# Preln attention with a mixture of experts: the last blocks' weighted sums turned by VectorE and DMA for three of eight token blocks

## The chip, the cores and the metric

The kernel runs on one core of one Trainium2 chip. The metric is the device time of one launch in microseconds (us), the median of several runs of the same program. TensorE (PE) multiplies matrices, VectorE (DVE), ScalarE (ACT) and GpSimd (POOL) work on rows, and SP only issues DMA transfers. Each engine takes its instructions in the order of the built program and waits on semaphores.

## The reference

Input x has 4096 tokens of width 256, in float32. Two residual steps follow each other:

```python
x = x + attention(layernorm(x), Qw, Kw, Vw)        # causal, one head of width 256
x = x + moe(layernorm(x))

h      = x @ W_in + b_in
probs  = softmax(h @ W_gate + b_gate)              # 8 experts, the best 2, shares normalized
mid    = relu(h @ W1[e] + b1[e])                   # 256 -> 1024
eout   = mid @ W2[e] + b2[e]                       # 1024 -> 256
out    = (share0 * eout0 + share1 * eout1) @ W_out + b_out
```

## The kernel before, in words

Tokens are cut into 8 blocks of 512 (NB blocks of TB), each of 4 tiles of 128 rows (TPB). The first half of the program is the attention, block by block. The second half gathers the rows of each expert from DRAM, computes `mid` and `eout` for groups of rows in one long list of work (`work`), and scatters each row's result to a DRAM array `parts`, two rows for a token, by indirect DMA on GpSimd's queue (line 997, in `contribute`). The last group of that list is called z: its rows are those of one expert from the last two token blocks.

The change concerns the end, where each token's two results are fetched, weighted, summed and multiplied by W_out. Four functions do it for a block b:

- `collect(b)` (line 1155) issues the loads of the block's rows from `parts` on SP's queue: two tiles `yp` of 512 KB (four of 256 KB for block 0). The two tiles use the buffers of pools `kt` and `v`, 8 each, in which the experts' weights were.
- `add_up(b)` (line 1170) makes the weighted sums `acc`, for each tile of 128 rows one product on ScalarE (line 1175) and one multiply-add on VectorE (line 1177).
- `gather(b)` (line 1187) calls `add_up` for every block but 0, turns the sums by 8 transposes of 128x128 on TensorE into two PSUM tiles `pa` (line 1195), and copies these by ScalarE into two tiles `aT` (line 1200). Here width runs along the partitions, as the next product wants it.
- `leave(b, aT)` (line 1203) multiplies by W_out, 2 matmuls for each of the 4 tiles, into PSUM tiles `pf` (line 1209), of which there are 4; VectorE adds the residual (line 1217, `ot`), and SP issues the output (line 1222; line 1219 for the last block).

A float32 matmul appears as two records in the profile, a float32 transpose as one.

The loads of blocks 0 to 5 are issued while the last group z is computed. Blocks 6 and 7 need z's scattered rows, so their loads come after it; SP's queue is in order, so everything issued later on SP stands behind them. Then the loop runs: `gather(b + 1)`, `leave(b)`. The order of instructions is that of the calls where they are pinned (`pin` and `keep_in_program_order` fix an instruction's place after the one before it on its engine); elsewhere a scheduler that estimates durations sets it when the program is built. In the program before, it interleaves the transposes of block b + 1 with the matmuls of block b on TensorE, and the sums of block b + 1 with the output additions of block b on VectorE.

In the attention part some blocks of layer-normed rows are already turned without TensorE: `turn_todo` (line 323) transposes 32x32 squares in place on VectorE, two instructions of 128x512 (line 329), and then moves the squares to their partitions by 16 transfers of 32 KB on SP's queue (line 334).

SP's transfers take eight completion semaphores in turn. Each issue waits until the last transfer on its semaphore has landed. GpSimd's queue does the same with eight of its own.

Of the kernel before, what the change touches and what calls it, by code (L numbers as in the profile page):

```python
# [10 lines left out]
F32 = mybir.dt.float32  # L11
# [6 lines left out]
P = 128  # L18
EPS = 1e-5
MASKED = -1e38  # L20
TB = 512
# [7 lines left out]
SQ = 32  # L29
LATE = 2  # L30
# [7 lines left out]
def preln_attention_moe_kernel(  # L38
# [249 lines left out]
    def first_rows():  # L288

        todo, keep = [], tc.keep_in_program_order  # L290
        z = ln_rows(0, 0, todo)
        for i in range(TPB // 2):
            for j in range(2):
                ln_stats(0, 2 * i + j, keep)
            ln_rstd(0, i, 2, keep)
        for do in todo:
            keep(do())
        return z
# [21 lines left out]
            for q in range(P // SQ)  # L320
        ]

    def turn_todo(zT, z):

        def stand(i):
            on = z[:, ts(i, TPB // 2), :]
            return nc.vector.transpose(on, on)

        def move():
            for q in range(P // SQ):
                for f in range(P // SQ):
                    nc.sync.dma_start(
                        out=zT[ts(f, SQ), :, :, ts(q, SQ)].rearrange("p j c i -> p (j c) i"),
                        in_=z[ts(q, SQ)].rearrange("p j (c f) -> p (j c) f", f=P)[
                            :, :, ts(f, SQ)
                        ],
                    )

        return [partial(stand, i) for i in range(2)] + [move]
# [7 lines left out]
    share = [const.tile([P, NT], F32, tag=f"share{k}", name=f"share{k}") for k in range(TOPK)]  # L349
# [123 lines left out]
    qT = {}  # L473
# [412 lines left out]
    def pin(done):  # L886
        if steady:
            tc.keep_in_program_order(done)
# [127 lines left out]
    z, gates = first_rows(), []  # L1016
# [62 lines left out]
    for g in range(NT // KU):  # L1079
        b, q = divmod(g, QPB)  # L1080
# [58 lines left out]
        if q == QPB - 1:  # L1139
            ln_rstd(1, b)  # L1140
            z1T = attn.tile([P, TPB, ND, P], F32, tag="z1T", name=f"z1T{b}", bufs=1)
# [8 lines left out]
                    do()  # L1150

    HT = TPB // 2
    yps, accs = {}, {}

    def collect(b):

# [10 lines left out]
                    tc.add_to_no_dep_group("out", get.ins)  # L1167
            yps[b, i] = yp

    def add_up(b):  # L1170
        for i in range(2):
            acc = accs[b, i] = piece(f"acc{b}_{i}", HT, D)
            for j in range(HT):
                t = b * TPB + i * HT + j
                pin(nc.scalar.mul(acc[:, j, :], yps[b, i][:, j, 0, :], share[0][:, t : t + 1]))
                pin(
                    nc.vector.scalar_tensor_tensor(
                        acc[:, j, :],
                        yps[b, i][:, j, 1, :],
                        share[1][:, t : t + 1],  # L1180
                        acc[:, j, :],
                        ALU.mult,
                        ALU.add,
                    )
                )

    def gather(b):

        pts = [ps_tr(f"pa{b}_{c}") for c in range(ND)]
        if b > 0:  # L1190
            add_up(b)
        for i in range(2):
            for j in range(HT):
                for c in range(ND):
                    nc.tensor.transpose(
                        pts[c][:, ts(i * HT + j, P)], accs[b, i][:, j, ts(c, P)], ident
                    )
        aT = [piece(f"aT{b}_{c}", TB) for c in range(ND)]
        for c in range(ND):
            nc.scalar.copy(aT[c], pts[c])  # L1200
        return aT

    def leave(b, aT):
        for i in range(2):
            ot = piece(f"ot{b}_{i}", HT, D)
            for j in range(HT):
                pf = ps_mm(f"pf{b}_{i}_{j}")
                for c in range(ND):
                    nc.tensor.matmul(  # L1209
                        pf[:, :D],  # L1210
                        lhsT=aT[c][:, ts(i * HT + j, P)],
                        rhs=wout_sb[:, c, :],
                        start=(c == 0),
                        stop=(c == ND - 1),
                    )
                t = i * HT + j
                nc.vector.tensor_tensor(ot[:, j, :], pf[:, :D], xb[b][:, t, :], ALU.add)
                if b == NB - 1:
                    nc.sync.dma_start(out=outs[b * TPB + t], in_=ot[:, j, :])
            if b < NB - 1:  # L1220
                t = b * TPB + i * HT
                nc.sync.dma_start(out=outs[t : t + HT].rearrange("t p d -> p t d"), in_=ot)
# [5 lines left out]
    for n, item in enumerate(work):  # L1228
        steady = n >= AHEAD
        if n == AHEAD:  # L1230
            take_late()
            quarters_left = nc.values_load(
                tables["d"][3][:1, :1],
                min_val=0,
                max_val=2 * NPAIR,
                skip_runtime_bounds_check_because="the sum of the experts' quarters",
            )

        if n + AHEAD + 1 < len(work):
# [13 lines left out]
        following = None  # L1253
        if n + 2 < len(work):
            following, behind = hidden(work[n + 1], got[n + 1], hTs.pop(n + 1), behind)
        if n == 0:
            turn(1, NB - 1, rows1, z1T)
            lg = enter(NB - 1, z1T, attn)
        if n == 1:
            seen = route(NB - 1, lg, seen, attn)  # L1260
            tables["z"], seen = plan_late(seen, early)
            tables["b"] = plan("b", seen, NBLK - NFULL, SB, SQR - 1, tables["a"][2])

            def twice(k):
                taken = const.tile([P, NE], F32, tag="twice" + k, name="twice" + k)
                nc.vector.tensor_scalar_mul(taken, tables[k][2], 2.0)
                return taken

            tables["c"] = plan("c", seen, NHALF, SH, SQR - 1, twice("b"))
            tables["d"] = plan("d", seen, 2 * NPAIR, SQR, SQR - 1, twice("c"))  # L1270
        if n == len(work) - 1:

            for b in range(NB - LATE):
                collect(b)
            add_up(0)
        contribute(item, got.pop(n), mid)
# [12 lines left out]
    steady = False  # L1289
    for b in range(NB - LATE, NB):  # L1290
        collect(b)

    aT = gather(0)
    for b in range(NB):
        following = gather(b + 1) if b + 1 < NB else None
        leave(b, aT)
        aT = following


# [30 lines left out]
```

## Time and profile before

| what | value |
| --- | --- |
| median of 3 runs | 1080.48 us (1079.9 to 1081.41) |
| the profiled execution's own time | 1071.75 us |
| its span, first to last instruction | 1070.0 us |
| granted TensorE clock | 1.000 |
| TensorE busy | 1062.3 us, 99% |
| VectorE busy | 674.6 us, 63% |
| last multiplication group z, first weighted sums | from 1017.25 us, from 1024.8 us |
| products with W_out (pf) | 1032.7 to 1066.4 us |

The profile is of one execution, whose own time is 8.7 us below the median of the runs. The span starts with its first instruction, and all positions are in us from there. A row of the chain gives start, length, engine, tile and line. A row of a tile's answer gives line, engine, operation, count, and the shortest, median and longest duration in ns. A row of SP's waits gives the line that waited, what for, the total in us, how often, and the longest. "Idle before" an instruction is in square brackets in a timeline, with what ended it.

In the end stretch, the busy time in each 8 us is:

```
us               PE    DVE   ACT   POOL  DMA share
1022 to 1030     8.00  2.10  3.33  0.98  0.99
1030 to 1038     7.43  3.80  4.64  0.98  1.05
1038 to 1046     8.00  5.94  5.15  0.00  0.99
1046 to 1054     8.00  5.81  4.67  0.00  0.73
1054 to 1062     8.00  6.22  4.67  0.00  0.37
1062 to 1070     4.80  2.55  0.62  0.00  0.38
```

### The profile page before, as it was taken

The page shows a single profiled execution, that of the slowest core. Times are in us where ns is not written, and L with a number is a line of the kernel's source. Part 1 is how long each engine was busy: PE and PEld are TensorE (multiplying, and loading weights), DVE is VectorE, ACT ScalarE, POOL GpSimd, SP SyncE. Part 2 cuts the span into 40 slices and gives each one's busy share as a digit, 9 for nine tenths or more (in the row PEclk, how much of TensorE's full clock was granted, in tenths as well). Part 3 has the DMA queues.
Part 4 walks back from the last instruction along what each step waited for, and adds up shares of the span by engine and source line. Part 5 has one row for each costly group of instructions (what it writes and reads, how often), then busy time and mean ns, then how long its engine had stood idle before and what let it go on. Part 6 is the DMA issues. An engine that isn't in the chain of part 4 may idle for free.

```text
span 1070.0 us, 15770 instructions
## 1 busy us (share of the span) xinstructions
PE 1062.3 (99%) x4973; PEld 882.9 (83%) x4973; DVE 674.6 (63%) x2114; ACT 332.4 (31%) x730; POOL 236.9 (22%) x289
## 2 busy tenths in 40 slices
PE   9999999999999999999999999999999999999998
PEld 6788888888888888888888887777778787777887
DVE  5877667564655546254665724858588786767636
ACT  2232233322432323242402221232323332323254
POOL 2104043103103000201222522232322322313110
PEclk9999999999999999999999999999999999999999
DMA  9422211121011011001655475887889896969285
GB/s 313 104 54 44 58 25 51 17 54 24 6 45 25 8 21 39 3 1 21 202 170 180 124 248 180 280 266 268 279 269 315 262 333 213 335 211 327 77 300 187
DMA packets 177995, 158.80 MB, mean 148 GB/s; under 512 B 82158, under 2 KB 157875, under 8 KB 177909
## 3 DMA queue, kind: packets, MB, share of 16 engines
q1 hardware_dynamic: 168980, 139.67, 42.4%
q0 software_dynamic: 8384, 17.58, 5.1%
q8 instruction: 40, 0.66, 0.3%
q10 hardware_dynamic: 544, 0.52, 0.1%
q14 instruction: 47, 0.38, 0.1%
HBM read 124.79 MB, written 26.38 MB: 141 GB/s over the span
## 4 chain that ended last, share of the span: by engine, by line
PE 97%; DVE 2%; POOL 0%; DMA 0%; issue 0%; SPq 0%; ACT 0%; DVEq 0%; POOLq 0%
PE po L633 21%; PE ps L555 21%; PE pm_a L921 11%; PE pe_a L988 11%; PE pe_b L988 5%; PE pm_b L921 5%; PE ph L362 3%; PE pm_c L951 3%; PE pf L1209 3%; PE pe_c L988 3%; PE pq L511 3%; PE pv L526 2%; PE pe_d L988 2%; PE pm_d L951 2%; PE pm_z L921 1%; PE pe_z L988 1%
## 5 line engine op out<-in xcount | busy, mean ns | idle before, releaser
L633 PE MATMUL po<-v,s 128*128 128x257 f32 x1056 | 237.9, 380 | 0.0
L555 PE MATMUL ps<-qT,zT 128*128 128x256 f32 x1088 | 233.3, 374 | 0.0
L555 PEld LDWEIGHTS ps<-qT,zT 128*128 128x128 f32 x1088 | 203.1, 190 | 28.0 <-issue 1.0
L633 PEld LDWEIGHTS po<-v,s 128*128 128x128 f32 x1056 | 197.2, 190 | 26.7
L564 ACT COPY s<-ps 128x512 f32<-128x512 f32 x120 | 70.2, 585 | 171.9 <-PE ps L555 132.6
L988 PE MATMUL pe_a<-w_a,mid_a 128*128 128x256 f32 x544 | 121.6, 380 | 0.0
L921 PE MATMUL pm_a<-hT_a,w_a 128*128 128x256 f32 x544 | 120.0, 379 | 0.0
L988 PEld LDWEIGHTS pe_a<-w_a,mid_a 128*128 128x128 f32 x544 | 102.6, 190 | 19.0 <-issue 5.6
L570 DVE TENSOR_TENSOR mx<-ps,mx 128x512 f32<-128x512 f32 x91 | 62.9, 691 | 83.7 <-ACT s L564 82.9
L930 ACT ACTIVATE mid_a<-pm_a,c_a 128x256 f32<-128x256 f32 x136 | 64.2, 472 | 165.1 <-PE pm_a L921 150.4
L921 PEld LDWEIGHTS pm_a<-hT_a,w_a 128*128 128x128 f32 x544 | 103.4, 190 | 14.1
L615 ACT ACTIVATE s<-s 128x512 f32<-128x512 f32 x120 | 72.2, 630 | 100.2 <-DVE s L612 100.2
L901 DVE STREAM_TRANSPOSE hT_a<-h_a 32x128 f32<-32x128 f32 x272 | 82.2, 302 | 3.8
L443 POOL DMA_INDIRECT slots<-assign,ati x64 | 62.5, 977 | 77.5 <-DVE ati L441 58.7
L612 DVE TENSOR_TENSOR s<-s,pmax 128x512 f32<-128x512 f32 x120 | 73.0, 679 | 7.3 <-PE pmax L608 7.3
L997 POOL DMA_INDIRECT parts<-y_a,slot_a x34 | 34.2, 1005 | 167.4 <-DVE y_a L996 138.0
L893 DVE STREAM_TRANSPOSE mid_c<-raw_c 32x256 f32<-32x256 f32 x128 | 55.8, 436 | 1.9
L988 PE MATMUL pe_b<-w_b,mid_b 128*128 128x256 f32 x256 | 56.8, 380 | 0.0
L921 PE MATMUL pm_b<-hT_b,w_b 128*128 128x256 f32 x256 | 56.6, 379 | 0.0
L988 PEld LDWEIGHTS pe_b<-w_b,mid_b 128*128 128x128 f32 x256 | 48.5, 190 | 9.4 <-issue 2.8
L921 PEld LDWEIGHTS pm_b<-hT_b,w_b 128*128 128x128 f32 x256 | 48.6, 190 | 6.6
L930 ACT ACTIVATE mid_b<-pm_b,c_b 128x256 f32<-128x256 f32 x64 | 30.1, 470 | 63.0 <-PE pm_b L921 63.0
(280 smaller groups left out, 1163.5 us busy)
## 6 DMA issues: line engine op xcount, KB each, us to landing
w_a<-in_L_ffn_W_dram SPq DMA_DIRECT2D x68, 512.0 KB, 6.0
w_d<-in_L_ffn_W_dram SPq DMA_DIRECT2D x48, 512.0 KB, 6.8
w_c<-in_L_ffn_W_dram SPq DMA_DIRECT2D x32, 512.0 KB, 8.1
w_b<-in_L_ffn_W_dram SPq DMA_DIRECT2D x32, 512.0 KB, 7.8
rows<-hr SPq DMA_DIRECT2D x16, 512.0 KB, 3.2
yp<-parts SPq DMA_DIRECT2D x14, 512.0 KB, 7.0
x<-in_L_attn_x_dram SPq DMA_DIRECT2D x7, 512.0 KB, 4.2
z1T<-z SPq DMA_DIRECT2D x112, 32.0 KB, 2.0
```

The costliest lines, as they stand in the source:

```text
L443: put = nc.gpsimd.indirect_dma_start(out=slots, out_offset=bass.IndirectOffsetOnAxis(ap=ati[:, j : j + 1], axis=0), in_=assign[:, TOPK * ( ...
L555: nc.tensor.matmul(ps[:, u * QB + lo : (u + 1) * QB], lhsT=zT[kt // TPB][:, kt % TPB, d, :], rhs=qT[b][:, d, q * QB + lo : (q + 1) * QB], ...
L564: nc.scalar.copy(flat, ps)
L570: done = nc.vector.tensor_tensor(mx, ps, old, ALU.max)
L612: nc.vector.tensor_tensor(s, s, pm[:, :QB].unsqueeze(1).to_broadcast([P, KU, QB]), ALU.subtract)
L615: nc.scalar.activation(s, s, AF.Exp)
L633: nc.tensor.matmul(po[u][:, : D + 1], lhsT=ss[c][:, k, ts(u, P)], rhs=vb[kt // TPB][:, kt % TPB, :], start=(kt == 0), stop=(kt == g * KU + u),
L893: pin(do())
L901: pin(do())
L921: nc.tensor.matmul(pm[:, :SB], lhsT=w1[c][:, ts(f, P)], rhs=hT[:, c, :], start=(c == 0), stop=(c == ND - 1),)
L930: nc.scalar.activation(mid[f // 2][:, f % 2, :], pm[:, :SB], AF.Relu, bias=c1[:, f : f + 1])
L988: nc.tensor.matmul(pe[ts(j, rest), :D], lhsT=mid[f][:, ts(u, P)][:, ts(j, rest)], rhs=w2[f // (NF // 2)][:, f % (NF // 2), :], start=(f == 0),
```

## The change

The sums of blocks 3, 5 and 7 are no longer turned by TensorE and copied by ScalarE. They are made in one tile each (`sum`, in the buffers of the layer-normed rows, tags z0 and z1), turned by VectorE's two instructions in place and moved by 16 transfers, of which every third starting with the second goes to GpSimd's queue: 11 on SP and 5 on GpSimd. The result goes to the buffers tagged qT (blocks 3 and 5) or z1T (block 7), and `leave` reads it from there.

The sequence changes with it. The loads of the first six blocks are issued in the sequence 0, 3, 1, 2, 5, 4, and those of the last two as 7, 6. The sums of block 3 are made straight after those of block 0, ahead of the additions of group z. The transfers of block 3 are issued before the loads of blocks 7 and 6. Block 1's sums are made in a pinned place after block 3's transposes. The sums of blocks 5 and 7 are pinned: after `gather(2)` and ahead of `leave(1)`, and after `gather(4)` and ahead of `leave(3)`; their transposes and transfers follow that `leave`.

```diff
-    def turn_todo(zT, z):
+    def turn_todo(zT, z, queues=(nc.sync,)):
...
-                    nc.sync.dma_start(
+                    queues[(q * P // SQ + f) % len(queues)].dma_start(
...
+    EARLY = [0, 3, 1, 2, 5, 4]
...
-    def add_up(b):
+    def add_up(b, home=None, keep=pin):
         for i in range(2):
-            acc = accs[b, i] = piece(f"acc{b}_{i}", HT, D)
+            acc = piece(f"acc{b}_{i}", HT, D) if home is None else home[:, ts(i, HT), :]
+            accs[b, i] = acc
...
+    def add_up_apart(b, keep=tc.keep_in_program_order):
+
+        home = attn.tile([P, TPB, D], F32, tag=f"z{b // 2 % 2}", name=f"sum{b}", bufs=1)
+        add_up(b, home, keep)
+        accs[b] = home
+
+    def turn_sums(b):
+        tag, bufs = ("z1T", 1) if b == NB - 1 else ("qT", 2)
+        aT = attn.tile([P, TPB, ND, P], F32, tag=tag, name=f"aT{b}", bufs=bufs)
+        for do in turn_todo(aT, accs[b], (nc.sync, nc.gpsimd, nc.sync)):
+            done = do()
+            if done:
+                tc.keep_in_program_order(done)
+        turned[b] = aT.rearrange("p j c t -> p c j t")
+
     def gather(b):
 
+        if b in turned:
+            return turned.pop(b)
         pts = [ps_tr(f"pa{b}_{c}") for c in range(ND)]
-        if b > 0:
+        if b > 1:
             add_up(b)
...
-                        lhsT=aT[c][:, ts(i * HT + j, P)],
+                        lhsT=aT[:, c, i * HT + j, :] if dma else aT[c][:, i * HT + j, :],
...
-            for b in range(NB - LATE):
+            for b in EARLY:
                 collect(b)
             add_up(0)
+            add_up_apart(3, pin)
...
-    for b in range(NB - LATE, NB):
+    aT = gather(0)
+    turn_sums(3)
+    add_up(1, None, tc.keep_in_program_order)
+    for b in (7, 6):
         collect(b)
-
-    aT = gather(0)
     for b in range(NB):
         following = gather(b + 1) if b + 1 < NB else None
+        if b in (1, 3):
+            add_up_apart(b + 4)
         leave(b, aT)
+        if b in (1, 3):
+            turn_sums(b + 4)
         aT = following
```

More of the change, by code (lines that the diff above doesn't have):

```diff
@@ L1152, in preln_attention_moe_kernel @@
     HT = TPB // 2
-    yps, accs = {}, {}
+    EARLY = [0, 3, 1, 2, 5, 4]
+    assert NB - LATE == len(EARLY)
+    yps, accs, turned = {}, {}, {}
     def collect(b):
@@ L1168, in collect @@
             yps[b, i] = yp
-    def add_up(b):
+    def add_up(b, home=None, keep=pin):
         for i in range(2):
-            acc = accs[b, i] = piece(f"acc{b}_{i}", HT, D)
+            acc = piece(f"acc{b}_{i}", HT, D) if home is None else home[:, ts(i, HT), :]
+            accs[b, i] = acc
             for j in range(HT):
                 t = b * TPB + i * HT + j
-                pin(nc.scalar.mul(acc[:, j, :], yps[b, i][:, j, 0, :], share[0][:, t : t + 1]))
-                pin(
+                keep(nc.scalar.mul(acc[:, j, :], yps[b, i][:, j, 0, :], share[0][:, t : t + 1]))
+                keep(
                     nc.vector.scalar_tensor_tensor(
@@ L1197, in gather @@
                     )
-        aT = [piece(f"aT{b}_{c}", TB) for c in range(ND)]
+        aT = [piece(f"aT{b}_{c}", TPB, P) for c in range(ND)]
         for c in range(ND):
-            nc.scalar.copy(aT[c], pts[c])
+            nc.scalar.copy(aT[c].rearrange("p j t -> p (j t)"), pts[c])
         return aT
     def leave(b, aT):
+        dma = not isinstance(aT, list)
         for i in range(2):
```

## The prediction

> **What bounds the kernel now.** I read the page's busy shares first, then the chain that ended last, then, for the last 40 us (the only stretch in which the change adds, removes or moves anything), the chain in order of time, the tiles concerned, VectorE's timeline and the waits of SP's queue. The page first: busy time by engine, and the chain's shares.
>
> ```profile
> PE 1062.3 (99%) x4973; PEld 882.9 (83%) x4973; DVE 674.6 (63%) x2114; ACT 332.4 (31%) x730; POOL 236.9 (22%) x289
> PE 97%; DVE 2%; POOL 0%; DMA 0%; issue 0%; SPq 0%; ACT 0%; DVEq 0%; POOLq 0%
> ```
>
> TensorE is busy all along, so work taken from it is worth its full time, unless a wait grows in its place. The chain in order of time, over the end:
>
> ```profile
> 1031.31 0.78 PE pa L1195 x7
> 1032.09 0.02 issue
> 1032.11 0.59 ACT aT L1200
> 1032.70 0.04 issue
> 1032.75 1.99 PE pf L1209 x8
> ...
> 1061.40 0.22 PE pa L1195 x2
> 1061.62 5.20 PE pf L1209 x24
> 1066.82 0.02 issue
> 1066.84 0.42 DVE ot L1217
> ```
>
> From 1032.75 to 1066.8 there is nothing but pa (the transposes) and pf (the products with W_out): TensorE never waits. A record of pf takes 5.20 / 24 = 0.216 us of it, one of pa 0.22 / 2 = 0.11. A block is 16 pf (3.46) and 8 pa (0.87). Three tile answers give the neighbours' prices, and VectorE's timeline shows why TensorE need not wait:
>
> ```profile
> L1177 DVE SCALAR_TENSOR_TENSOR acc<-yp,share,acc x32: 473/477/486, 1025.3 to 1060.3; 128x256 f32<-128x256 f32 x32
> L329 DVE STREAM_TRANSPOSE z<-z x26: 666/701/708, 36.4 to 488.8; 128x512 f32<-128x512 f32 x26
> L334 SPq DMA_DIRECT2D z1T<-z x112: 585/609/1556, 50.0 to 499.4; - x112
> ```
>
> ```profile
> 1041.44 0.48 DVE L1177 SCALAR_TENSOR_TENSOR acc<-yp,share,acc 128x256 f32<-128x256 f32 x1 [0.17 <-ACT acc L1175]
> 1041.84 0.41 DVE L1217 TENSOR_TENSOR ot<-pf,x 128x256 f32<-128x256 f32 x1
> 1042.18 1.26 DVE L1177 SCALAR_TENSOR_TENSOR acc<-yp,share,acc 128x256 f32<-128x256 f32 x3
> ```
>
> VectorE makes the next block's sums between two output additions, and TensorE turns each as it comes (pa x2 among the pf records). Successive sums start 0.40 apart, successive output additions 0.33 to 0.40. Last, SP's waits in the end stretch:
>
> ```profile
> SPq L1165 <- DMA parts<-y_z,late_slot: 7.0, 1, 7.0
> SPq L1165 <- DMA parts<-y_b,slot_b: 3.3, 1, 3.3
> SPq L1165 <- DMA yp<-parts: 1.8, 3, 0.9
> ```
>
> The third row matters: a load of partial results waited for an earlier one. SP's transfers take eight completion semaphores in turn, so each issue waits until the transfer eight places before it has landed. The DMA engines are 0.99 to 1.05 busy from 1022 to 1046 (table by windows), so landings are late there: the first fourteen loads were issued by 1030.2, but in the trace the thirteenth landed at 1039.4 and the fourteenth at 1040.6.
>
> [...] the large loads of SP's queue land one behind the other, 1.3 to 1.7 us apart. [...] The kernel has no direct transfer on that queue; the nearest row is the scatter of 128 rows, 0.98 us.
>
> **The change, part by part.** *Removed.* Blocks 3, 5 and 7 lose 8 transposes each: 24 x 0.109 = 2.62 us of TensorE, on the path. Their 6 copies on ScalarE (0.59 each) go too; ScalarE is not the limit (4.7 busy of 8 us), so nothing for that.
>
> *Added on VectorE.* 6 transposes of 0.70. Block 3's pair follows y_z at 1031.77, and VectorE was idle until 1033.62: free. Block 3's sums now stand ahead of y_z and wait for the second pair of loads (landed 1027.65 and 1029.4): y_z's first half slips from 1027.9 to some 1030.4 and its scatter by about 2; TensorE wants that PSUM buffer at 1031.2: hidden, by under 1 us. If not, the loss is what it is late by.
>
> *Moved: the sequence on VectorE and TensorE.* Here the built program's order decides, as both engines take their instructions in order. VectorE gets, after block 1's third output addition: four sums of block 5, the fourth addition of block 1, the two transposes of block 5, four additions of block 2, and only then the sums of block 4. TensorE gets all of block 2's pf and then the transposes of block 4, each waiting for its sum; before, they were interleaved. Walk it: sums of block 5 from 1041.44 (ScalarE's place is unchanged) to 1043.1; addition 1043.5; transposes (2 x 0.70 less overlap) 1044.8; four additions 1046.1; first sum of block 4 at 1046.6, the last at 1047.75. TensorE, unhindered, is at 1032.75 + 2 x 4.33 + 3.46 = 1044.87 and would leave the transposes at 1045.74; it leaves them at 1048.0. Loss 2.2 us. Behind it: block 3's and 4's pf end at 1054.95. On VectorE, after block 3's fourth addition (1051.9), two sums of block 7, its two transposes (1054.0), block 4's additions (the last after pf, 1055.4), then block 6's sums from 1055.9: transposes of block 6 end at 1057.3 in place of 1055.8. Loss 1.5 us.
>
> *Moved and added: the queues.* Each turn brings 16 transfers of 32 KB: 11 on SP, 5 on GpSimd. SP's cost 0.65 apart (16 in 10.4 us at 489.6) and land 2.0 after issue. They go between other transfers of SP: block 3's before the loads of blocks 7 and 6, block 5's after the outputs of blocks 0 and 1, block 7's after those of 2 and 3.
> - Block 3: from 1033.2, but the eighth waits for the semaphore of the fourteenth load (1040.6), the ninth for the first of its own kind, queued behind those loads: last issue 1042.6, landed by 1044.6 to 1045.5. Wanted at 1048.0: hidden.
> - Loads of blocks 7 and 6: issued 1043.2 to 1044.7 (before: 1037.8 to 1039.3), landed some 1047 to 1050.7. Wanted from 1049 and 1051: about hidden.
> - Outputs of blocks 0 and 1: 1045.2 to 1046.5, queued behind those loads, landing 1051.4 to 1053.5.
> - Block 5: first issue 1046.9, but its fourth waits for the last load (1050.7), the fifth to eighth for the outputs (to 1053.5), then 3 x 0.65: last issue 1055.5, landed 1057.5. Wanted at 1057.3: loss 0.2 at most.
> - Block 7: turned by 1054.0, but SP first issues four outputs (4 x 0.42) and then 11 x 0.65: last issue 1064.3, landed 1066.4. TensorE is through blocks 5 and 6 at 1057.3 + 6.92 = 1064.2. Loss 2.2.
>
> GpSimd's part is unknown: five issues per block. By the nearest row 1.0 us each (one scatter has half the runs: 256 of 128 bytes here); upper bound 2.0, if the cost goes with the runs. Below 1.0 gains nothing, as SP's part lands later. At 1.0 block 7's are issued by 1059.3 and land in time; at 2.0 they are issued by 1064.3, and land 2 to 5.5 us after (5.5 is what the last scatters took under load). I take 1.0 to 1.5. Behind them in that queue stands only the end of the program.
>
> Sum: -2.62 + 2.2 + 1.5 + 2.2 = +3.3 us, and about 0.2 because the outputs of blocks 4 to 6 stand behind block 7's transfers and are still draining at the end: +3.5. The profiled execution (1071.75, span 1070.0) becomes 1075.2. The median shown is 8.7 above that execution; I carry the difference over: 1080.48 + 3.5 = **1084.0 us**. A change under 0.2% (2.2 us) can't be told from none here.
>
> **Rivals.**
> *SP's chain is hidden, only VectorE's order costs.* If the semaphores come free earlier, block 7 is on time: -2.62 + 3.7 = +1.1, 1081.6. For it: 33 + 12 issues alone take 27 us from 1033.2, in time without waits; against it: full DMA engines to 1046. It decides if block 5's last issue comes before 1053.3 in place of 1055.5.
> *Faster: VectorE keeps up.* TensorE gets its 2.62 us: 1077.9. The one mechanism is the 5.2 us of VectorE's work between 1041.4 and block 4's first sum; it would have to fit in 3.5 us. VectorE is idle a quarter of the time here (5.8 to 6.2 busy of 8 us), which speaks for it; the order and the durations speak against.
> *GpSimd is the last to deliver.* At 2.0 us an issue block 7 lands at 1066.4 to 1069.8, TensorE waits up to 5.6 us: +3.5 to +6.9, up to 1087.4.
>
> **How the numbers follow.** Likeliest case 0.5 (its own range 1082.4 to 1086), SP hidden 0.2, faster 0.1, GpSimd late 0.2. The range leaves out the faster case and GpSimd's worst: 1080.3 to 1087.5. Slower by over 0.2%: nine tenths of the first and all of the last, 0.64; same: most of the second and some of the first, 0.23; faster 0.13.
>
> **What would show it.** Idle time of TensorE before pa of block 4 (about 1.7, then thrice 0.2) and of block 6, ended by VectorE's sums; idle time before block 7's pf, ended by a transfer; SP's waits for its own earlier transfers up from 1.8 to 5 or more; pa x40 in place of x64; GpSimd's issues near 1.0. The prediction is wrong if TensorE's last 34 us have no such gaps, if landings on SP come earlier than walked, or if turned sums of block 3 or 5 are late too.

## The result, and the profile after

The changed kernel takes 1091.92 us (median of five executions, 1090.42 to 1093.36) against 1080.48 for the kernel before: ratio 1.0103, 95% interval 1.0090 to 1.0117. It is 11.4 us slower; forecast were 3.5. The direction was right, the size was not: the time lies above the forecast's range of 1080.3 to 1087.5.

The page of the changed kernel (profiled execution 1093.36, span 1091.6), busy time of TensorE and the shares of the chain that ended last:

```profile
PE 1070.5 (98%) x4949; PEld 886.5 (81%) x4949; DVE 680.9 (62%) x2120; ACT 330.1 (30%) x724; POOL 245.8 (23%) x304
PE 93%; another core or an unknown queue 2%; DVE 2%; DMA 2%; issue 0%; ACT 0%; POOL 0%; SPq 0%; ACTq 0%; DVEq 0%; POOLq 0%
```

TensorE has 24 instructions fewer and yet 8 us more of busy time: its records have become longer. And the chain now has DMA in it, and "another core or an unknown queue", of which below. The two profiled executions can't be compared over their whole span: the first record of pf begins at 1032.75 before and at 1043.74 after, 10.99 us later, in a part of the kernel that the change doesn't touch. So I compare the end stretch, from the first pa to the last pf, and what follows it.

The changed kernel's chain in order of time (start, length, what), from block 4's sums to the last product:

```profile
1056.55 0.41 DVE ot L1239
1056.96 0.40 DVE acc L1181
1057.36 0.14 issue
1057.49 1.53 PE pa L1216 x8
1059.03 0.23 issue
1059.26 1.90 PE pf L1231 x4
...
1061.34 8.84 DMA out_dram<-ot
1070.17 0.02 issue
1070.19 0.58 SPq L334
...
1072.13 1.99 DMA aT<-sum
1074.11 0.14 issue
1074.25 13.40 PE pf L1231 x48
```

Read it from below. The last 48 pf (blocks 5, 6, 7) wait until 1074.1 for a transfer of block 5, issued at 1072.13, the last of eleven on SP. The chain goes on through an output of block 1, issued at 1061.34 and landed 8.84 us later, because one of the eleven needed its completion semaphore. But that was only the last of the holds, and a short one. SP's waits while it issued the eleven (from 1061 to 1073 us; line, waited for: total, times, longest):

```profile
SPq L334 <- DMA yp<-parts: 2.7, 3, 1.3
SPq L334 <- DMA out_dram<-ot: 0.4, 1, 0.4
```

The loads of blocks 7 and 6 held them for 2.7 us and the outputs for 0.4. The rest of the 10.1 us from the first of the eleven (1062.01) to the last is the issues themselves, at 0.65 us or more each. TensorE's timeline (start, length, what, and in brackets the idle time before it and what ended it) shows the four places where it stands:

```profile
1057.49 1.53 PE L1216 MATMUL pa<-ident,acc 128*128 128x128 f32 x8 [1.37 <-DVE acc L1181]
1059.26 8.83 PE L1231 MATMUL pf<-wout,aT 128*128 128x256 f32 x32 [0.23 <-issue]
1069.09 1.53 PE L1216 MATMUL pa<-ident,acc 128*128 128x128 f32 x8 [1.00 <-DVE acc L1181]
1074.25 13.39 PE L1231 MATMUL pf<-wout,aT 128*128 128x256 f32 x48 [3.63 <-DMA aT<-sum]
```

At the old price of 0.216 us a record, 32 pf are 6.92 us and 48 are 10.37; here they take 8.83 and 13.39. The table by windows (window, length, busy time and records of PE, PEld, DVE, ACT and POOL, granted clock, DMA share, GB/s) says why:

```profile
1056.10:1059.40 3.30, 1.70 (x10) 0.98 (x10) 2.43 (x7) 0.39 (x1) 2.87 (x5) 1.00 0.56 87
1059.40:1062.80 3.40, 3.40 (x9) 2.69 (x10) 0.42 (x1) 1.53 (x4) 0.00 (x0) 0.50 0.99 321
1062.80:1069.70 6.90, 5.90 (x29) 4.72 (x27) 6.52 (x17) 2.78 (x7) 1.16 (x2) 1.00 1.08 327
1069.70:1073.10 3.40, 0.92 (x6) 0.40 (x4) 0.43 (x2) 1.07 (x2) 1.73 (x3) 1.00 0.53 84
1073.10:1079.90 6.80, 5.65 (x13) 4.55 (x14) 1.00 (x3) 0.00 (x0) 0.00 (x0) 0.50 0.69 186
```

Twice TensorE is granted half its clock, each time behind a window in which it was idle for about half the time or more. In the kernel before, the clock is 1.00 throughout the end stretch. The sum of the two profiles:

| term, us | forecast | measured |
|---|---|---|
| 24 transposes less | -2.62 | -2.62 |
| wait before pa of block 4 (1.37, and 8 pa spread over 1.53 in place of 0.87) | +2.2 | +2.03 |
| wait before pa of block 6 (1.00 + 0.66) | +1.5 | +1.66 |
| wait before pf of block 5 | at most 0.2 | +3.63 |
| wait before pf of block 7 | +2.2 | 0 |
| half clock (1.91 on 32 pf, 3.02 on 48) | not in it | +4.93 |
| small waits | 0 | +0.2 |
| from the last pf to the end (3.20 before, 3.96 after) | +0.2 | +0.76 |
| sum | +3.5 | +10.6 |

The end stretch itself is 35.66 us before and 45.50 after. With what follows it that makes 10.6, within the interval of the ratio (9.7 to 12.6 us). How it splits between waits and half clock changes from one execution to the next: the term of half clock is 4.93 us here and 2.7 in a second profile of the changed kernel, shown below, where the end stretch is 46.27 us.

### The profile page after: what moved, and what is told of

Same layout as the page of the kernel before. It is cut to its first block, busy times and chain, and to the rows that moved or that the text cites. A ratio compares the mean times of both kernels' runs of the same rounds, so it can differ in the third digit from the quotient of the medians.

```text
span 1091.6 us, 15786 instructions
## 1 busy us (share of the span) xinstructions
PE 1070.5 (98%) x4949; PEld 886.5 (81%) x4949; DVE 680.9 (62%) x2120; ACT 330.1 (30%) x724; POOL 245.8 (23%) x304
## 4 chain that ended last, share of the span: by engine, by line
PE 93%; another core or an unknown queue 2%; DVE 2%; DMA 2%; issue 0%; ACT 0%; POOL 0%; SPq 0%; ACTq 0%; DVEq 0%; POOLq 0%
PE po L633 20%; PE ps L555 20%; PE pm_a L921 11%; PE pe_a L988 10%; PE pe_b L988 5%; PE pm_b L921 5%; PE ph L362 3%; PE pm_c L951 3%; PE pq L511 3%; PE pe_c L988 3%; PE pv L526 2%; PE pe_d L988 2%; PE pm_d L951 2%; PE pf L1231 2%; DMA out_dram<-ot 1%
```

## The experiments

Two theories stood at the start. **Theory 1** is the forecast's: SP's queue, with its eight semaphores (in the profile after, its issues update eight in turn, 79 or 80 times each), delivers late, and VectorE's order makes pa of blocks 4 and 6 late; added to it now is that a wait brings half clock. Its **rival** ("theory 2" below) is that the DMA engines have too much to move. The kernel before took 1081.2 to 1081.6 us on the two chips that ran most of these, and 1071.6 on the two that ran the long runs, block 7 alone, the short gap and the two single copies; each ratio is to the kernel before on the same chip.

### The kernel before, once more

> The kernel before, unchanged, beside itself: a look at an ordinary execution of it, since the one shown was 8.7 us shorter than the median. All theories: 1080 to 1081 us. If the 8.7 us are waits of unknown origin in the middle of the kernel (the profile after has two, 7.5 us on VectorE and 14.1 us on ScalarE, each followed by a spell of half clock), such waits appear in this profile too and TensorE's last 34 us have no gap and clock 1.0. If instead the clock is lower throughout the end, the end stretch itself (first record of pa to the last of pf) is longer than 35.5 us.

1081.26 us, ratio 1.0004 (0.9995 to 1.0012). Its waits, VectorE and ScalarE (engine, line, waited for: total, times, longest):

```profile
DVE m L603 <- remote: 6.8, 1, 6.8
ACT mid_a L930 <- remote: 14.1, 1, 14.1
```

An ordinary execution on such a chip has these two waits, which no record explains, and TensorE loses by them 2.57 us at 98 and 2.84 at 613, each with 3.41 us of half clock (1.7 lost) near it: 8.8 in all. That is the 8.7 us between the first profile of the kernel before and its median. The changed kernel's profile has the same two waits (7.5 and 14.1). The end stretch is 35.66 us here too, so nothing of this belongs to the change, and carrying the difference over to the median was right. What the two waits are is open.

### Does a wait cost more than its length?

Into the kernel before, ahead of block 4's transposes:

```
+        if b == 4:
+            late = accs[4, 1].rearrange("p j d -> p (j d)")
+            for _ in range(6):      # 4 in the short gap
+                pin(nc.vector.tensor_tensor(late, late, late, ALU.max))
```

> The kernel before, with six VectorE operations of 128x512 (max of a tile with itself, 0.69 us each, 4.1 us together) between block 4's sums and its transposes, so that TensorE stands idle for some 3 to 4 us once. Theory 1 [...]: a spell at 0.5 follows the gap, and the time rises by the gap and 1.7 to 3.4 us more: 1085 to 1088 us. Rival (a wait costs its own length): clock stays 1.0, 1083 to 1084.5 us.

> As the long gap, with four VectorE operations in place of six: TensorE stands idle about 1.4 us less, for some 1 to 1.5 us in all. Theory 1 [...]: clock stays 1.0 in the end stretch, 1081.8 to 1083.3 us. Rival (any gap brings a spell of half clock): 0.5 for 3.4 us and 1083.5 us or more.

Six operations: 1086.03 us, ratio 1.0047 (1.0034 to 1.0061). Four: 1073.42 us beside 1071.57, ratio 1.0017 (1.0010 to 1.0024). The windows around the gap (columns as above), six first:

```profile
1056.90:1061.00 4.10, 1.30 (x8) 0.79 (x7) 3.49 (x8) 1.19 (x3) 0.00 (x0) 1.00 0.18 60
1061.10:1064.40 3.30, 3.30 (x11) 2.66 (x11) 2.44 (x6) 1.38 (x4) 0.00 (x0) 0.50 0.38 126
```

```profile
1049.80:1052.00 2.20, 0.86 (x6) 0.55 (x6) 2.09 (x6) 0.77 (x2) 0.00 (x0) 1.00 0.13 46
1052.00:1055.40 3.40, 3.40 (x20) 2.88 (x21) 2.34 (x6) 2.15 (x6) 0.00 (x0) 1.00 0.47 159
```

With six, TensorE is idle for 2.80 us within 4.1 and a spell of 3.41 us at half clock follows; with four it is idle for 1.34 and none follows. The end stretches are 40.67 and 37.53 us, 3.14 apart: two operations are 1.38 of it, and half of 3.41 is 1.71. So half clock can follow a wait, and is charged on top of it. Theory 1's addition holds, and its rival (a wait costs its length) falls.

A wait's length alone does not decide it. In the profile after, the spells of half clock begin at 100.28, 619.11, 1059.42 and 1073.08 us, 152, 129 and 4 times 3.413 us apart, as if on a fixed grid of windows. The wait at 98 us shows what that does. In the kernel before, run once more (first three rows), it left TensorE idle for 2.57 us; in the sequence without the turning, the next experiment (last two rows), for 3.30:

```profile
94.90:98.30 3.40, 3.08 (x16) 2.33 (x14) 0.00 (x0) 0.00 (x0) 2.49 (x4) 1.00 0.41 56
98.30:101.70 3.40, 1.15 (x7) 1.04 (x8) 1.10 (x3) 0.00 (x0) 0.70 (x1) 1.00 0.13 18
101.70:105.10 3.40, 3.40 (x9) 2.33 (x8) 3.08 (x9) 3.29 (x7) 0.00 (x0) 0.50 0.00 0
96.10:99.50 3.40, 1.95 (x10) 1.33 (x9) 0.00 (x0) 0.00 (x0) 2.33 (x3) 1.00 0.37 53
99.50:103.00 3.50, 1.65 (x9) 1.50 (x10) 1.61 (x3) 0.40 (x1) 0.00 (x0) 1.00 0.02 2
```

The shorter wait put 2.25 us of idle time into one window, and half clock followed. The longer one was split, about 1.5 and 1.8 us, and none followed. The four operations' 1.34 us were split too, about 0.5 and 0.85, so they say little about where the limit lies.

### The sequence without the turning

```
     def turn_sums(b):
+        if b not in (-1, -2):      # no block is
+            return
...
-        if b > 1:
+        if b not in (0, 1, 3, 5, 7):
             add_up(b)
```

> The change's new sequence (loads in the order 0, 3, 1, 2, 5, 4, 7, 6; sums of 3, 5, 7 apart and early), but TensorE turns all eight blocks and nothing is turned by VectorE or DMA. Theory 1 (VectorE's transposes and the transfers make the waits): no wait of TensorE over 1 us in the end stretch, clock 1.0 there, 1080 to 1082 us. Rival (the sequence itself costs, as VectorE does the apart sums ahead of those of blocks 4 and 6): waits of 1 to 2 us before pa of block 4 and of block 6 stay and a spell of half clock follows, 1084 to 1088 us.

1081.38 us, ratio 1.0000 (0.9992 to 1.0008). The one wait over 1 us in the end stretch is at its start, on TensorE's timeline:

```profile
1040.69 0.98 PE L1218 MATMUL pa<-ident,acc 128*128 128x128 f32 x7 [1.22 <-DVE y_z L996]
```

The loads' new order and the early sums cost nothing that the times show. In this profile, though, the end stretch is 37.17 us, 1.5 longer than in the kernel before, and what makes up for it is luck: the wait at 98 us brought no half clock here (1.7 us less). So the sequence may cost up to some 1.5 us where y_z comes late for block 0, as here (by 0.82 us with block 5 alone turned); the forecast had it hidden by under 1 us. In the changed kernel y_z is not on the chain.

### One block at a time

The same kernel with `return` for all blocks but one (`(5, -2)` in place of `(-1, -2)` for block 5).

> The changed kernel's sequence, with block 3 alone turned by VectorE and DMA; TensorE turns the other seven. Theory 1a: block 3's transfers still push the loads of 7 and 6 back by about 8 us, but nothing of block 5's or 7's stands behind them; sums of 7 come at most 1 us late and TensorE waits under 1.5 us in all: 1080 to 1082.5 us (8 transposes, 0.87 us, saved). Rival (block 3's turn alone makes the waits): 1085 us or more.

> The changed kernel's sequence, with block 5 alone turned by VectorE and DMA. Theory 1a (block 5 is late because of block 3's transfers in front of the loads): block 5 arrives in time, no wait before its pf; the wait before pa of block 4 stays at 1 to 2 us as VectorE's two transposes stand in front of block 4's sums, perhaps with one spell of half clock (1.7 us): 1080.5 to 1084 us. Rival (block 5's own transfers are too slow): wait of 2 us or more before its pf, 1085 us or more.

> The changed kernel's sequence, with block 7 alone turned by VectorE and DMA. Theory 2 (the costs of the three blocks do not add: each alone finds room on the DMA engines, together they do not): block 7 arrives in time, VectorE's transposes in front of block 6's sums cost up to 1.5 us: 1080.5 to 1083.5 us; the three blocks alone then sum to 6 to 8 us over the kernel before, and the change to 10.5 or more. Rival (the costs add): block 7 alone costs 4.5 us or more, 1085.5 us or more.

Block 3: 1084.84 us, ratio 1.0039 (1.0025 to 1.0054). Block 5: 1083.53, 1.0023 (1.0015 to 1.0030). Block 7: 1071.77 beside 1071.57, 1.0005 (0.9997 to 1.0014). As ratios they sum to 0.7%, some 7 us, against 1.0% of all three; the intervals leave room for a sum of 0.4 to 1.0%, so that the three do more harm together than one by one is likely, but not shown. Block 3 missed what was expected of it, but not all of its 3.5 us is block 3's: its end stretch is 37.22 us, 1.6 over the kernel before, and some 2.0 us were lost ahead of it, where the change touches nothing. There the wait at 98 us was followed by 6.83 us of half clock in place of 3.41, which is 1.7 us; the first profile of the changed kernel has the same. Block 7 alone meets no wait:

```profile
1056.65 9.10 PE pf L1233 x42
```

In this chain the last 42 pf run without a stop, and the end stretch is 34.88 us, 0.8 shorter than before. But the time is the same: from the last pf to the end it takes 4.16 us in place of 3.20, as the last outputs land behind block 7's transfers. I moved the outputs of blocks 5 and 6 to ScalarE's queue to get this back:

```
+                (nc.sync if b < 5 else nc.scalar).dma_start(...)
```

> Block 7 alone turned by VectorE and DMA, as in e9_turn7, and the outputs of blocks 5 and 6 issued by ScalarE, which is idle by then, so that the last outputs don't queue behind block 7's transfers on SP. Theory (in e9_turn7 TensorE ended 0.8 us earlier in its end stretch, and the outputs gave it back): the stretch from the last pf to the end of the span goes from 4.2 us back to about 3.2, 0.5 to 1 us faster than before: ratio 0.999 to 0.9997. Rival (the landing of the last transfers is the same whatever the queue): ratio 1.000 to 1.001.

1082.08 us, ratio 1.0004 (0.9996 to 1.0012). The tail fell to 3.44 us as expected, but the end stretch is 35.53 again, with 0.43 us of waiting ahead of block 7's pf. A miss: what was saved at one place was given back at the other.

### Moving what stands in front of block 5

First the outputs of blocks 0 to 3 went to ScalarE's queue, then, from the changed kernel again, the loads of 7 and 6 to GpSimd's:

```
+                (nc.scalar if b < 4 else nc.sync).dma_start(out=outs[...], in_=ot)
```

```
+                queue = nc.sync if b < NB - LATE else nc.gpsimd
+                get = queue.dma_start(out=yp[...], in_=part[...])
```

> The changed kernel, but the eight output transfers of blocks 0 to 3 are issued by ScalarE on its own queue[...]. Theory 1 (block 5's eleven transfers wait for semaphores that the loads of 7 and 6 and the outputs hold): block 5's last issue comes about 4 us earlier, TensorE's wait before pf of block 5 falls from 3.6 us to under 1, the second spell of half clock goes or shortens: 1084.5 to 1088.5 us. Rival (the DMA engines are full and the data would be late in any queue): wait still 3 us or more, 1090.5 to 1093 us.

> The changed kernel, but the four loads of blocks 7 and 6 are issued by GpSimd (behind its five transfers of block 3) and no longer by SP behind its eleven. Theory 1a (the loads of 7 and 6 come 9 us late because they stand behind block 3's transfers, and they hold up everything behind them in SP's queue): loads issued at about 1049 in place of 1057 on the clock of the profile after, block 5's transfers landed by 1069, TensorE's wait before pf of block 5 falls from 3.6 us to under 1; the waits before pa of blocks 4 and 6 stay (2 and 1.5 us): 1083.5 to 1087.5 us. Rival (the DMA engines have too much to move in these 14 us, whatever the order): the wait before block 5 stays at 2.5 us or more, 1089.5 us or more.

Outputs: 1093.67 us, ratio 1.0112 (1.0095 to 1.0128). Loads: 1090.94, 1.0091 (1.0075 to 1.0106). Neither gain came. With the outputs on another queue the wait before block 5 was still 2.48 us, and before pa of block 6 it was 1.86, since the loads of block 7, and so the sums that VectorE makes first, were later (landed at 1062.9 and 1065.6 in place of 1061.7 and 1063.4, though this execution was 1.4 us ahead at the first pf). The 0.4 us that SP waited for outputs says why there was little to gain; and issued by ScalarE, one of them still held a transfer of SP's for 2.1 us (`SPq L334 <- DMA out_dram<-ot: 2.1, 1, 2.1`). With the loads on GpSimd's queue, TensorE's timeline:

```profile
1063.25 8.63 PE L1232 MATMUL pf<-wout,aT 128*128 128x256 f32 x32 [4.22 <-DMA aT<-sum]
...
1083.38 3.69 PE L1232 MATMUL pf<-wout,aT 128*128 128x256 f32 x16 [2.02 <-DMA aT<-sum]
```

Block 5's wait is gone as theory 1a said (0.20 is left), but block 3 is now 4.22 us late and block 7 2.02: loads and transfers changed places. With the loads beside them on another queue, block 3's last transfer on SP, issued at 1056.2 (1056.5 in the changed kernel), landed at 1062.8 in place of 1058.6.

Then VectorE's part was taken away as well, with the loads on GpSimd: pa of blocks 4 and 6 called for before the output additions of blocks 2 and 4.

```
+        if b in (2, 4):
+            ready[b + 2] = gather(b + 2)
...
         leave(b, ready.pop(b))
```

> As e4_loads_pool, and the sums of blocks 4 and 6 with their transposes are called for ahead of the output additions of blocks 2 and 4, so VectorE makes them right behind the transposes of 5 and 7. Theory 1: the waits before pa of blocks 4 and 6 shrink from 2.0 and 1.7 us to under 1 each, no spell of half clock: 1079.5 to 1083 us. Rival (VectorE has too much to do whatever its order): waits move to pf of blocks 2 and 4, which then wait for PSUM buffers: 1084 us or more.

1093.17 us, ratio 1.0111 (1.0092 to 1.0130). No gap before pa any more (the eight of block 4 are still spread over 1.53 us), and yet:

```profile
1061.84 5.83 PE L1232 MATMUL pf<-wout,aT 128*128 128x256 f32 x18 [5.13 <-DMA aT<-sum]
...
1081.89 5.38 PE L1232 MATMUL pf<-wout,aT 128*128 128x256 f32 x16 [3.41 <-DMA aT<-sum]
```

TensorE, early at block 3, only waits longer there. So VectorE's order was not what held the end.

Last, the outputs of blocks 0 to 3 were held back in SP's own queue until the transfers of block 5 (or 7) had been issued, beside the changed kernel once more on the same chip:

```
-                nc.sync.dma_start(out=outs[...], in_=ot)
+                held.append((outs[...], ot))
...
             turn_sums(b + 4)
+            put_held()
```

> The changed kernel, but SP issues the outputs of blocks 0 and 1 behind block 5's transfers and those of blocks 2 and 3 behind block 7's, in place of ahead of them. Theory 1 (what stands ahead in SP's queue sets block 5's landing): block 5's last issue no longer waits for outputs that land 4 us after the last load; TensorE's wait before pf of block 5 falls from 3.6 us to under 1.2 and with it one spell of half clock: 4 to 7 us faster than the changed kernel, ratio to before 1.003 to 1.007. Rival, theory 2 (the DMA engines are full, the order doesn't matter): wait of 2.5 us or more, ratio 1.0085 or more.

> The changed kernel again, beside e11_outs_behind on the same chip. Theory: ratio 1.009 to 1.012, waits of TensorE of some 8 us and two or three spells of half clock in the end stretch, in the same places as in the profile after. If the ratio is below 1.008 the chips differ, and the runs with moved queues and long runs have to be read against this one.

The change again (the second profile): 1092.42 us, ratio 1.0100 (1.0084 to 1.0115). Outputs held back: 1094.39 us, 1.0116 (1.0101 to 1.0132). TensorE's timelines, the change first:

```profile
1058.88 7.15 PE L1231 MATMUL pf<-wout,aT 128*128 128x256 f32 x32 [0.99 <-DMA aT<-sum]
...
1072.41 9.60 PE L1231 MATMUL pf<-wout,aT 128*128 128x256 f32 x32 [3.68 <-DMA aT<-sum]
1083.46 3.69 PE L1231 MATMUL pf<-wout,aT 128*128 128x256 f32 x16 [1.45 <-DMA aT<-sum]
```

```profile
1070.96 8.83 PE L1238 MATMUL pf<-wout,aT 128*128 128x256 f32 x32 [1.92 <-DMA aT<-sum]
1082.54 3.69 PE L1238 MATMUL pf<-wout,aT 128*128 128x256 f32 x16 [2.74 <-DMA aT<-sum]
```

Block 5's wait falls from 3.68 to 1.92, so what stood ahead of it in the queue did hold it; block 7's rises from 1.45 to 2.74. The end stretch is 45.30 us, 1.0 shorter, but the outputs held back land late: from the last pf to the end it takes 6.6 us in place of 4.0. It is the fourth rearrangement that moved a wait and saved nothing.

### Taking the transfers' cost away

Keep number, size, queue and order of the 48 transfers, but copy straight across in longer runs:

```
-        for do in turn_todo(aT, accs[b], (nc.sync, nc.gpsimd, nc.sync)):
...
+        for n in range(16):
+            q, f = divmod(n, 4)
+            (nc.sync, nc.gpsimd, nc.sync)[n % 3].dma_start(
+                out=to[ts(q, SQ), ts(f, 256)], in_=of[ts(q, SQ), ts(f, 256)])
```

> The changed kernel, its 48 transfers of 32 KB kept in number, size, queue and order, but each copies 32 runs of 1024 bytes straight across in place of 256 runs of 128 bytes; the sums of blocks 3, 5 and 7 are so not turned, which this kernel leaves out. Theory 2 (the transfers' time on the DMA engines is what is missing: in the profile after, pieces of 128 bytes took 15 ns on average, so the 48 transfers take 10 us of all 16 engines, in a stretch where these are full; pieces of 1024 bytes took 47 ns, which makes 4.5 us): landings come 2 to 4 us earlier, TensorE's wait before pf of block 5 falls from 3.6 us to under 2 and there is less half clock: 1083 to 1088.5 us. Rival, theory 1 (the number of transfers and the eight semaphores set it): unchanged within 1.5 us of the changed kernel, 1090 us or more.

1080.57 us beside 1071.57: ratio 1.0081 (1.0068 to 1.0095). By the packet records of the traces, the 48 transfers take 10.0 us of all 16 DMA engines in the changed kernel (8448 pieces of 128 bytes at 15 ns on SP's queue, 240 of 2048 bytes at 137 ns on GpSimd's) and about 5 to 6 here (on SP's queue these pieces can't be told from those of the outputs). That brought some 2 us, and even this is not clear of the changed kernel's interval; the wait before block 5 fell from 3.63 to 2.69 us only. Theory 2 explains a part at most.

Then one straight copy of 512 KB per block, and the same with VectorE's early sums:

```
+        nc.sync.dma_start(out=aT.rearrange("p j c i -> p (j c i)"),
+                          in_=accs[b].rearrange("p j d -> p (j d)"))
```

> The changed kernel, with the sixteen transfers of each turned block replaced by one straight copy of 512 KB on SP; the sums of blocks 3, 5 and 7 are so not turned, which this kernel leaves out. VectorE's transposes, sums and their order stay. Theory (transfers and VectorE's order both cost): no wait before pf of blocks 3, 5 and 7; the waits before pa of blocks 4 and 6 stay (2.0 and 1.7 us), with at most one or two spells of half clock (1.7 us each): ratio to before 1.001 to 1.005. Rival 1 (the transfers cost everything): no wait over 0.5 us, ratio 0.998 to 0.9995. Rival 2 (VectorE's order costs nearly everything): ratio 1.0075 or more.

> As e14_one_copy (the sums of blocks 3, 5 and 7 are not turned either), with the sums of blocks 4 and 6 called for ahead of the output additions of blocks 2 and 4 as in e7_loads_sums. Theory: waits before pa of blocks 4 and 6 under 0.5 us each, no half clock; the 24 transposes' 2.6 us are left as gain, less what the waits keep: ratio 0.9975 to 0.9995. Rival (something else in the change costs, such as the loads' order or y_z's delay): ratio 1.001 or more.

One copy: 1070.06 us beside 1071.58, ratio 0.9986 (0.9980 to 0.9993). With early sums: 1070.81, 0.9994 (0.9986 to 1.0003). The single copies' timeline, around the sums of block 4 and the products of blocks 4 and 5:

```profile
1046.91 0.60 PE L1217 MATMUL pa<-ident,acc 128*128 128x128 f32 x4
1047.35 0.60 PE L1232 MATMUL pf<-wout,aT 128*128 128x256 f32 x2
...
1053.46 1.99 PE L1232 MATMUL pf<-wout,aT 128*128 128x256 f32 x8 [0.33 <-DVE ot L1240]
```

Beside the 0.57 us before the first pf, which the kernel before has too, the 0.33 shown is the longest wait left, and there is no half clock: end stretch 33.77 us, 1.9 shorter than before. VectorE's work and its order are unchanged, so rival 1 of this run holds: the transfers cost it all, from 1.0103 to 0.9986, some 12.5 us. But one thing moved along: the program was built with half of block 3's pf ahead of pa of block 4 on TensorE (in the long runs too), and half of block 5's ahead of pa of block 6 (not in the long runs), so that TensorE has work until VectorE's sums come. In the changed kernel pa of block 4 stands ahead of block 3's pf. The version with early sums keeps the changed kernel's order there; its eight pa of block 4 follow pf without a gap and are spread over 1.53 us, and no other wait comes near that.

What these runs settle: the transfers are the cause, not the sequence (some 1.5 us at most) and not VectorE by itself, and no place in the queues for the 48 of them was found that saves it. With their number unchanged, about half the engine time saved little; with one in place of sixteen, which still takes 3.9 us of all DMA engines, everything. So most of it goes with their number, that is with issues of 0.65 us each and with semaphores that come free only at a landing. SP's queue shows how: the loads of 7 and 6 were issued from 1037.8 us in the kernel before and from 1037.6 with single copies, but from 1044.6 in the long runs, behind eleven issues and their waits, and from 1046.2 in the changed kernel (10.99 subtracted). How it splits exactly between number and engine time is open, since TensorE's order changed in both of these runs and the changed kernel was not run on their chips. Not tried were fewer and larger transfers that still turn, and transfers on ScalarE's queue. No version that does the whole work was faster than the kernel before.

## Why the prediction was wrong, point by point

**What failed.** Two steps failed together. SP's queue was walked with landings that were too early, as if the 48 transfers took the DMA engines no time; and a wait of TensorE was counted at its length, without the half clock that can follow it. The forecast's sum has 2.2 us for the first and nothing for the second. In the profile after, they took 3.63 and 4.93 us; in the second profile 6.1 (waits of 0.99, 3.68 and 1.45 before pf of blocks 3, 5 and 7) and 2.7. That is 6.4 us more than forecast, of the 7.1 by which its sum is short, and 6.6 of 7.9 in the second profile.

**What bounds the kernel, and the 24 transposes.** Right: pa is x40, the saving is there, and it shows as 1.9 us of end stretch where the transfers are made cheap.

**VectorE's order before pa of block 4.** Right: forecast to be left at 1048.0, which is 1059.0 on the later clock of the profile after (10.99 added); the chain has 1057.49 + 1.53 = 1059.02. What the forecast did not see is that VectorE's lateness costs only because TensorE's order has no other work there: in the single copies it had, and did not wait.

**Before pa of block 6.** Forecast 1.5, measured 1.66, though both engines came there 2.3 us later than walked.

**SP's queue: the first step that failed.** The mechanism was right (SP's issues wait for landings, 6.3 us in all for those of loads; the issues at 1050.66, 1053.22 and 1054.59 began 0.01 to 0.02 us after the transfers eight places before them had landed, at 1050.64, 1053.20 and 1054.58), its times were not. I took the landings of the early loads from the kernel before, and put no time of the DMA engines to the 48 transfers, though the forecast itself had these engines full. By the completion events of the trace, each stage slipped further:

| us | forecast + 10.99 | measured |
|---|---|---|
| fourteenth load landed | 1051.6 | 1054.6 |
| loads of 7 and 6 issued | 1054.2 to 1055.7 | 1057.2 to 1058.9 |
| these landed | 1058.0 to 1061.7 | 1061.7 to 1066.6 |
| outputs of blocks 0 and 1 landed | 1062.4 to 1064.5 | 1067.3 to 1070.2 |
| block 5's last transfer landed | 1068.5 | 1074.1 |

Three microseconds at the first line are up to five at the third and almost six at the last. At the first line, block 3's transfers made one to two of the three: without them the fourteenth load landed 21.6 and 22.0 us after the first was issued (block 5 alone, sequence alone), in the changed kernel 23.6, in the kernel before 20.6. The rest came with the new sequence. SP's waits for loads are the trace's own sum of the delay: up from 1.8 us in all to 7.1, most of it in one row.

```profile
SPq L334 <- DMA yp<-parts: 6.3, 6, 2.0
```

**Where it would bite.** Forecast were 0.2 us at block 5 and 2.2 at block 7; measured 3.63 and 0 (3.68 and 1.45 in the second profile). TensorE, stopped at block 5, reached block 7 late enough to find it there in the first profile; in the second it waited 1.45 us for it as well. Block 3, forecast to have landed more than 2 us early, came 0.6 us before TensorE wanted it, and 0.99 late in the second profile. Late turned sums of block 3 or 5 were one of the forecast's own signs of being wrong.

**GpSimd's issues.** Wrong, without effect: forecast 1.0 to 1.5 us each, measured 0.58, less than SP's 0.61. The nearest row of the kernel before, the scatter on GpSimd's queue, was 0.98. GpSimd's issues update eight semaphores of their own, 26 or 27 times each.

```profile
L334 POOL DMA_DIRECT2D aT<-sum x15: 582/582/684, 1044.8 to 1071.8; - x15
```

**The clock: the second step that failed, missing altogether.** 4.93 us, the largest term of this profile, came from half clock behind the waits (4.5 by the clock's own records, half of the 3.40 and 5.65 us that TensorE was busy in the two spells; the rest comes from how records overlap behind a stop: at full clock, too, 32 pf took 7.15 us there in place of 6.92). The forecast counted a wait by its length, and the profile before, at a granted clock of 1.000, showed no half clock. The two spells of the end stretch are 3.41 and 6.83 us long, and TensorE was idle for 1.60 and 2.46 us of the 3.41 us before them.

**The outputs' tail.** Forecast 0.2, measured 0.76.

**The rivals.** SP hidden, and VectorE keeping up, are refuted by the chain: block 5's last issue, which had to come before 1053.3 for the first, came at 1072.13, which is 1061.1 on the forecast's clock. GpSimd last to deliver didn't happen. The true case, late at block 5 and half clock behind, was on no list; the range's upper end, 1087.5, had only GpSimd's lateness in it.

## What to carry to other kernels

Before work is moved from a full engine to DMA, add its transfers' issues, engine time and semaphores to the queue that carries them, and walk the landings again from the first one, not from the old trace: here a queue that was just full delivered everything behind it later and later. Where TensorE is the bound, price a wait at its length and at the half clock that may follow: here 1.60 to 2.46 us of idle time in one window of 3.41 us were followed by 3.41 or 6.83 us of it, 1.7 to 3.4 us on top. Whether it comes can hang on how the wait falls into the windows (3.30 us of idle time, split between two, brought none), so one profile can be lucky. And when a wait moves to another place each time that its apparent cause is taken away, stop rearranging and take the load itself away once, even in a kernel that leaves part of the work out: it tells in one run what the rearrangements can't.

## What the runs showed of the hardware

- In the profile after, spells of half clock are 3.41 or 6.83 us long and begin on a grid of 3.413 us. Counted by that grid from 60 us to the last pf, half clock followed the full-clock windows in which TensorE was idle for 1.60, 2.16, 2.42 and 2.46 us, and none of the others, with 1.00 us or less. At half clock a second window at half followed on 0.91 and 1.17 us of idle time, and none on no idle time. In the kernel before, run once more, 2.25 us in one window brought a spell; in the sequence without the turning, about 1.5 and 1.8 us in two windows brought none. What decides near 1.6 to 1.8 us these runs don't tell. So the same wait can cost its length or 1.7 to 3.4 us more: at 98 us a gap of 3.30 us brought no half clock, one of 2.57 brought 3.41 us of it, one of 3.34 (the profile after) brought 6.83.
- GpSimd issued a direct transfer of 32 KB with 256 runs in 0.58 us, SP in 0.61. Its fifteen show as 240 pieces of 2048 bytes at 137 ns on average, SP's thirty-three as 8448 of 128 bytes at 15 ns; per transfer that is 2.2 us of one engine on GpSimd's queue and 3.9 on SP's.
- On the chips where the kernel before takes 1081 us, its profile and those of the changed kernel had two waits that no record explains (some 7 us on VectorE at 93, 14.1 on ScalarE at 603), worth 8.8 us to TensorE in the kernel before; the profiles on the other two chips, where it takes 1071.6, had neither.
